# A GRU over 128 steps on one Trainium2 core: the last ten steps' units given out anew, weights of x reloaded into the room of weight sums, and one unit of each period moved behind the projection

## The chip, the core and the metric

The kernel runs on one core of a Trainium2 chip. Its engines work side by side, each on its own queue of instructions: TensorE (PE, matrix products, into PSUM banks), VectorE (DVE), ScalarE (ACT), GpSimd (POOL), and SyncE (SP), which here only issues DMAs. The metric is the device time of one execution in microseconds (us). The profiler also leaves one profiled execution with a trace of every engine.

## The reference

A GRU runs over 128 steps on a batch of 64 sequences with 512 features, in float32; after every fourth step but the last its state goes through one more layer, the projection. The result is added to x.

```python
def step(h, inp):
    x_t, prop = inp
    comb = jnp.concatenate([x_t, h], axis=-1)
    z = jax.nn.sigmoid(comb @ Wz + bz)
    r = jax.nn.sigmoid(comb @ Wr + br)
    comb2 = jnp.concatenate([x_t, r * h], axis=-1)
    h_cand = jnp.tanh(comb2 @ Wh + bh)
    h_new = (1.0 - z) * h + z * h_cand
    h_next = jnp.where(prop, jnp.tanh(h_new @ Wp + bp), h_new)
    return (h_next, h_new)
# prop: (t + 1) % 4 == 0 and t < T - 1; the outputs are the h_new
return x + gru(x, cond_1024, Wz, bz, Wr, br, Wh, bh, Wp, bp)
```

The weights Wz, Wr, Wh have 1024 rows: the upper 512 meet x, the lower 512 meet the state.

## The kernel before

**The recurrent part.** A step t needs three gates, R, Z and H_ (the candidate), and every fourth step (t = 3, 7, ...) the projection P_. The batch is cut into two halves of 32 sequences, h = 0 and 1, and `half(h)` is a generator that emits one half's steps one after the other. A gate of a half is four `products` of 256 columns over the state's transpose (`hT`, or `rhT` for the candidate, `hpT` behind a projection). The chain of a half through a step is: R's products; sigmoid on ACT (L806); r times h and its transpose on DVE (L807, L808); Z's products meanwhile; the candidate's products; tanh on ACT (L846); product with z, subtraction of `keep` and transpose on DVE (L848, L857, L858); in the fourth steps the projection's products, tanh and transpose (L872 to L876). `keep` and the sigmoid of z are made for both halves at once, behind the second half's Z (L818 to L823). A gate's PSUM region is seeded by ACT with the x part and the bias before its products come (`seed`, L368); the seeds of the next step stand on ACT behind the activations that read the regions (L810, L862, L864, L878), and the seed of Z waits for the second half's new state. The loop at L885 to L896 interleaves the halves by the columns that each has emitted, the second one 700 columns behind.

**The x part: units.** x times the upper weights for all steps is work that doesn't hang on the state. It is cut into units and stands in a `queue` (`put`, L383). `fill(n, h)` emits the next n units of a half at three places of a step, given by a triple in `places`: before the candidate's products (`places[0]`, L839), behind the candidate (`places[1]`, L866), and, in the fourth steps, behind the projection (`places[2]`, L880). So the units are what PE does while a chain is on ACT and DVE. Steps 0 to 4 take their triples from HEAD, the last ten from TAIL, the others from PLACES, a period of eight steps that begins with u = (t - 3) % 8 = 0 (steps 11, 19, ..., 115). A half-unit may not be emitted for h = 0 before the unit that frees its bank was emitted for h = 1 (`after` in `fill`).

**Two forms of units.** Most of x goes through a fast scheme of seven products per pair of steps, twice nested, in `batch`. It needs sums and differences of weights: `tw` (made once, read for the products 4, 6 and 7), `tt`, and differences that replace parts of `wx` in place in the first step (`sum_outer_1`, `sum_inner_1`). A batch is 14 units of 192 columns for two products (7 for one), in the order j = 2, 7, 1, 5, 4, 6, 3, in PSUM banks: a (j = 2), x or y (7, later 4 on top), q (1, later 6), r (5, later 3). Behind a bank's last unit stands its reader: `end_x` copies x or y to `cx` on ACT (L507), `end_q` and `end_q2` copy q to `cq` on ACT, `end_r` (L514, L515), `end_q2` (L520) and `end_r2` (L523, L524) add on DVE. Sums on POOL then make the x parts `cp` of the steps (`outer_...`, `pair_left`, `pair_right`). `plain_unit` is the other form: four products of 256 columns per gate and step against the original weights, followed by `add_bias` on DVE (L409). It is used for steps 0 to 3 and for the last two, T - 2 and T - 1.

**The end.** For the plain products of the last two steps, `wx` must hold the original weights again. `reload` (L455) loads rows k = 0 to 2 of it with twelve DMAs on SP in step T - 7 (L840); the rows k = 3 were never replaced, and `plain_last` puts the units with k = 3 first. The four steps from T - 4 on get their x part from two last batches (`pair_left`, `pair_right` with g = LAST, L687 to L690) and from the plain units. `behind_step` adds the state to x in `xr` on POOL (L765), stores finished steps (L775) and loads later x (L90), all on SP.

Of the kernel before, what the change touches and what calls it, by code (L numbers as in the profile page):

```python
# [9 lines left out]
F32 = mybir.dt.float32  # L10
# [8 lines left out]
def kernel(  # L19
# [15 lines left out]
    B, T, D = x.shape  # L35
    H = h0.shape[1]
    P = 128
# [34 lines left out]
    wh = [const.tile([P, K, H], F32, name=f"wh_{i}") for i in range(3)]  # L72
    wp = const.tile([P, K, H], F32, name="wp")

    tw = {n: const.tile([P, S, NQ, 3, J // 2], F32, name=f"tw_{n}") for n in (2, 3, 4)}
    tt = const.tile([P, 7, 3, NQ, 3, J // 4], F32, name="tt")
    gates_in = (Wr, Wz, Wh)

# [139 lines left out]
    def product(ps, h, lT, w, k, start=False):  # L218
        c0, s0 = divmod(k, C)
        products(  # L220
            ps.rearrange("p (d j) -> p d j", d=2),
            h,
            lT[:, c0, s0 * B + h * V : s0 * B + (h + 1) * V],
            lambda c: quarters(w)[:, c, k],
            start,
        )
# [175 lines left out]
    def banks(t):  # L402
        first, second = scratch[:2] if t % 2 == 0 else scratch[2:4]
        return (first[:, : S * J], first[:, S * J :], second[:, : S * J])

    def add_bias(t, gates):
        new_cp(t // 2)
        for i in gates:
            nc.vector.tensor_add(  # L409
                G[t][:, :, :, i, :],  # L410
                banks(t)[i].rearrange("p (h c n) -> p c h n", h=S, c=C),
                bias_x[:, :, :, i, :],
            )

    def plain_unit(t, e, k, start, end=None):
        g, i = divmod(t, Q4)
        bank = (q_bank, q_bank, r_bank) if t % 2 == 0 else (a_bank, a_bank, x_banks[0])
        return (
            lambda h: product(banks(t)[e], h, xT[g][:, i], wx[:, :, e, :], k, start and e != Z),
            S * J,  # L420
            bank[e],
            end,
            bank[1:] if end is not None else (),
        )

    def plain(t):
        order = [(e, k) for e in range(3) for k in range(K)]
        if t == Q4 - 1:
            order = [(e, k) for k in range(K) for e in range(3)]
        return [  # L430
            plain_unit(
                t, e, k, k == 0, (lambda: add_bias(t, (R, Z, H_))) if n == 11 else None
            )
            for n, (e, k) in enumerate(order)
        ]

    def plain_last():
        seq = [
            plain_unit(t, e, 3, True) for t in (T - 2, T - 1) for e in (R, Z, H_)
        ]  # L440
        for t, gates in ((T - 2, (R, Z, H_)), (T - 1, (R, Z)), (T - 1, (H_,))):
            order = [(e, k) for k in (2, 0, 1) for e in gates]
            seq += [
                plain_unit(
                    t,
                    e,
                    k,
                    False,
                    (lambda t=t, gates=gates: add_bias(t, gates)) if (e, k) == order[-1] else None,
                )  # L450
                for e, k in order
            ]
        return seq

    def reload():  # L455
        for i in range(3):
            load_w(wx[:, :, i, :], gates_in[i][:D], 0, 3)

    MB = {}

# [138 lines left out]
    def pair_right(a, p1, x_, g=1):  # L599
# [2 lines left out]


    PLACES = (
        (1, 8, 5), (1, 7, 0), (6, 8, 0), (6, 8, 0), (1, 8, 5), (1, 7, 0), (6, 8, 0), (6, 6, 0),
    )
    HEAD = {0: (12, 12, 0), 1: (8, 6, 0), 2: (16, 12, 0), 3: (8, 6, 8), 4: (6, 8, 0)}
    TAIL = {
        T - 10: (6, 4, 0), T - 9: (3, 8, 0), T - 8: (6, 8, 0), T - 7: (6, 6, 0), T - 6: (0, 4, 0),
        T - 5: (0, 3, 0), T - 4: (0, 3, 0), T - 3: (0, 5, 0), T - 2: (0, 3, 0), T - 1: (0, 0, 0),  # L610
    }

    idle(64)
# [43 lines left out]
    def begin(t):  # L657
        u = (t - 3) % 8
        even = FIRST + 2 * ((t - 3) // 8)
        if t == 0:  # L660
            put(plain(2) + plain(3))
        elif t == 1:
            put(batch((1, 0), [(1, 1), (1, 2)]))
        elif t == 2:
            put(batch((1, 1), [(1, 10), (1, 11)]) + batch((1, 2), [(1, 8), (1, 9)]))
        elif t == 3:
            put(batches(FIRST))
        elif u == 7:
            put(batches(even + 2))
        if t == T - 10:  # L670
            put(
                batch((LAST, 0), [(LAST, 1), (LAST, 2)])
                + batch((LAST, 1), [(LAST, 10)])
                + plain_last()
            )

    def behind_r(t, duo, u):
        odd = FIRST + 2 * duo + 1
        if t == 1:
            for i in (5, 7):  # L680
                sum_inner(i, nc.gpsimd)
                sum_inner_1(i, nc.gpsimd)
        if t == 2:
            pair_left(0, 1, 2)
        elif t == 3:
            pair_right(0, 1, 10)
        if t == T - 7:  # L687
            pair_left(0, 1, 2, LAST)
        elif t == T - 6:
            pair_right(0, 1, 10, LAST)  # L690
        if t == 2:
            sum_inner(4, nc.gpsimd)
            sum_inner_1(4, nc.gpsimd)
        if u == 0 and duo >= 1 and odd - 2 < LAST:
            outer_u2(odd - 2)
# [17 lines left out]
    def behind_step(t, duo, u, h_new):  # L713
        g, j = divmod(t, Q4)
        even, odd = FIRST + 2 * duo, FIRST + 2 * duo + 1
        if t == 0:
            join_x(1, 0)
            join_x(1, 1)
            sum_raw12(1)
        elif t == 3:  # L720
            pair_left(1, 8, 9)
            pair_right(1, 8, 11)

        if duo >= 0:
            if u == 0 and duo >= 1 and odd - 2 < LAST:
                outer_c22(odd - 2)
                outer_c21(odd - 2)
            if even * Q4 < T:
                if u == 0:
                    sum_s34(even)  # L730
                elif u == 1:
                    outer_1(even)
                    outer_c11(even)
                    sum_raw12(odd)
                elif u == 2:
                    outer_u1(even)
                    outer_5(even)
                    sum_raw4(even)
                elif u == 3:
                    outer_c12(even)  # L740
                    outer_u2(even)
                    outer_c22(even)
                    if odd < LAST:
                        sum_s12(odd)
                elif u == 4:
                    if odd < LAST:
                        sum_s34(odd)
                    outer_c21(even)
                    if odd < LAST:
                        outer_1(odd)  # L750
                elif u == 5 and odd < LAST:
                    sum_raw4(odd)
                elif u == 6 and odd < LAST:
                    outer_u1(odd)
                    outer_c11(odd)
                elif u == 7 and odd < LAST:
                    outer_5(odd)
                    outer_c12(odd)
        if duo >= -1 and (even + 2) * Q4 < T:
            if t == 2 or (u == 6 and duo >= 0):  # L760
                sum_raw12(even + 2)
            if u == 7:
                sum_s12(even + 2)
        if t < T - 1:
            nc.gpsimd.tensor_add(xr[g][:, j], xr[g][:, j], h_new)  # L765

        n = 0
        if t >= T - CHUNK:
            n = 3 if t == T - 2 else 0
        elif j == Q4 - 1:  # L770
            n = 4
        if n:
            for h in range(S):
                for q in range(NQ):
                    nc.sync.dma_start(  # L775
                        out=out[ts(h, V), t - n + 1 : t + 1, ts(q, J)],
                        in_=xr[g][part(q), j - n + 1 : j + 1, h, :],
                    )
        if j == 1 and g >= 1 and (g + 1) * Q4 < T:
            new_xr(g + 1)  # L780
            load_x(xr[g + 1], (g + 1) * Q4, Q4)
        if t in (1, 2):
            load_xs(t + 2)
        if duo >= 0:
            if u == 3:
                load_xs(odd + 2)
            elif u == 6:
                load_xs(even + 4)

    def half(h):  # L790

        for t in range(T):
# [13 lines left out]
            crossed(r_, h, R, AF.Sigmoid)  # L806
            nc.vector.tensor_mul(rh[:, h, :], r_, h_old[:, h, :])  # L807
            turn(rhT[:, h, :], rh[:, h, :])  # L808
            if t != 3:
                seed(R, t + 1, h)  # L810
            if last:
                seed(H_, t, h)
# [24 lines left out]
                    for n in range(2, 4):  # L837
                        join_x(2, n)
            yield from fill(places[0], h)  # L839
            if h == 1 and t == T - 7:  # L840
                reload()

            yield from gate(H_, h, rhT, wh[H_])
            h_new = new_two("h", t)
# [15 lines left out]
                nc.scalar.copy(gate_ps(P_, h)[ts(h, 2 * V)], bias_p[ts(h, 2 * V)])  # L860
            elif t < T - 2:
                seed(H_, t + 1, h)  # L862
            if h == 1:
                seed(Z, t + 1, 0)  # L864
            state[t + 1] = h_new, hT
            yield from fill(places[1], h)  # L866
            if h == 1 and t == 0:
                sum_outer_1()
                for i in (1, 2, 3):
                    sum_inner_1(i, nc.vector)  # L870
# [65 lines left out]
```

## Time and profile before

| | |
|---|---|
| runs | 1307.67, 1312.48, 1312.58 us (median 1312.48) |
| profiled execution | 1309.2 us, span from first to last instruction 1307.3 us |
| busy, DVE / ACT / POOL | 59% / 64% / 68% of the span |
| granted TensorE clock, mean | 0.993 |
| a period of eight steps (steps 11/12 to 19/20) | 78.04 us (172.10 to 250.13) |
| reload: first issue to the matmul that waits for it | 1246.89 to 1260.13 us |
| last matmul's end to the end of the span | 1301.44 to 1307.33 us |

In the profile's lines L12 is line 12 of the kernel, times are microseconds unless marked ns, `out<-in` are the program's names without buffer numbers, and a note such as `[0.91 <-ACT cx L497]` says how long the engine was idle before the instruction and which instruction ended that. L204 is the one line in `products` that issues all matmuls of gates, projections and units, so these are told apart by the tile they write: `rec` and `rec_z` for gates and projections, `scratch_q`, `scratch_r`, `scratch_a`, `scratch_x` and `scratch_y` for units.

### The profile page before, as it was taken

What the parts mean: (1) busy time and instruction counts of PE and PEld (TensorE: products, weight loads), DVE (VectorE), ACT (ScalarE), POOL (GpSimd) and SP (SyncE); (2) the same over time, 40 slices, a digit from 0 to 9 for tenths busy, and PEclk for the clock granted to TensorE, in tenths of its full rate; (3) what the DMA queues carried; (4) which work ended last, traced back from release to release, by engine and by line L of the source; (5) the groups of instructions that cost most, each with busy time, mean ns of one, the idle gap of its engine ahead of it and who ended that gap; (6) DMA issues with size and microseconds to landing.
All of it is one profiled execution on the core that took longest, in us unless ns stands there. A gap on an engine that the chain in (4) does not pass through costs nothing.

```text
span 1307.3 us, 60823 instructions
## 1 busy us (share of the span) xinstructions
PE 1263.1 (97%) x26024; PEld 1085.0 (83%) x26024; DVE 774.2 (59%) x2163; ACT 837.9 (64%) x2688; POOL 887.4 (68%) x1030
## 2 busy tenths in 40 slices
PE   7989999999999999999999999999999999999987
PEld 3579988888888888888888888888888888888855
DVE  1646666666665656666666565666656666666534
ACT  1346666666666666666666666666666666666655
POOL 4468767777677776767687676776767787676420
PEclk9989999999999999999999999999999999999999
DMA  8502211112121111211111121111112102111040
GB/s 190 111 19 52 51 35 39 47 35 51 42 61 35 27 46 48 51 36 47 45 30 51 47 56 36 34 48 40 51 36 55 41 25 51 51 36 35 19 107 18
DMA packets 114710, 63.19 MB, mean 48 GB/s; under 512 B 13161, under 2 KB 109673, under 8 KB 114441
## 3 DMA queue, kind: packets, MB, share of 16 engines
q1 hardware_dynamic: 113412, 58.44, 18.0%
q8 instruction: 205, 3.36, 1.1%
q10 hardware_dynamic: 772, 0.72, 0.2%
q14 instruction: 65, 0.52, 0.1%
q0 software_dynamic: 256, 0.14, 0.1%
HBM read 42.47 MB, written 16.78 MB: 45 GB/s over the span
## 4 chain that ended last, share of the span: by engine, by line
PE 88%; DMA 4%; DVE 2%; ACT 2%; SPq 2%; POOL 1%; issue 1%; DVEq 0%; POOLq 0%
PE rec L204 41%; PE rec_z L204 15%; PE scratch_r L204 13%; PE scratch_q L204 9%; PE scratch_a L204 4%; PE scratch_y L204 3%; PE scratch_x L204 3%; DMA xr<-in_x_dram 1%; DVE rec_z L848 1%; DVE h L857 1%; SPq L97 1%; ACT c L230 1%; DMA wx<-in_L_cond_Wz_dram 1%; DMA wh<-in_L_cond_Wr_dram 1%; ACT cx L497 1%
## 5 line engine op out<-in xcount | busy, mean ns | idle before, releaser
L204 PE MATMUL rec<-wh,rhT 128*32 128x256 f32 x4096 | 373.7, 381 | 4.4 <-ACT rec L371 4.4
L204 PE MATMUL rec<-wh,hT 128*32 128x256 f32 x3072 | 277.7, 379 | 2.1 <-DVE hT L233 2.1
L204 PE MATMUL rec_z<-wh,hT 128*32 128x256 f32 x3072 | 278.1, 379 | 0.0
L204 PEld LDWEIGHTS rec<-wh,rhT 128*32 128x32 f32 x4096 | 226.8, 110 | 38.9 <-ACT rec L371 4.8
L230 ACT ACTIVATE scratch_r<-rec 64x128 f32<-64x128 f32 x512 | 128.0, 250 | 146.2 <-PE rec L204 80.7
L371 ACT COPY rec<-cp 64x256 f32<-64x256 f32 x512 | 189.9, 371 | 31.6 <-DVE cp L409 7.7
L230 ACT ACTIVATE rec_z<-rec_z 64x128 f32<-64x128 f32 x512 | 128.0, 250 | 95.8 <-PE rec_z L204 83.6
L204 PEld LDWEIGHTS rec<-wh,hT 128*32 128x32 f32 x3072 | 167.2, 110 | 24.6 <-ACT c L230 3.7
L230 ACT ACTIVATE c<-rec 64x128 f32<-64x128 f32 x512 | 139.3, 272 | 66.8 <-PE rec L204 55.7
L204 PEld LDWEIGHTS rec_z<-wh,hT 128*32 128x32 f32 x3072 | 172.4, 110 | 8.2
L765 POOL TENSOR_TENSOR xr<-xr,h 128x256 f32<-128x256 f32 x127 | 93.2, 734 | 114.3 <-DVE h L857 109.0
L556 POOL TENSOR_TENSOR mb<-mb,mb 128x768 f32<-128x768 f32 x58 | 106.3, 1833 | 68.9 <-DVE mb L524 68.9
L556 POOL TENSOR_TENSOR cp<-mb,mb 128x768 f32<-128x768 f32 x75 | 137.4, 1831 | 5.5 <-DVE mb L524 1.9
L556 POOL TENSOR_TENSOR cp<-mb 128x768 f32<-128x768 f32 x47 | 86.1, 1832 | 56.4 <-ACT rec_z L371 54.9
L514 DVE TENSOR_TENSOR cx<-scratch_r,cx 128x384 f32<-128x384 f32 (+1 forms) x107 | 59.3, 554 | 106.2 <-PE scratch_r L204 97.6
L821 DVE SCALAR_TENSOR_TENSOR keep<-rec_z,h 128x256 f32<-128x256 f32 x96 | 40.8, 425 | 134.2 <-ACT rec_z L230 134.2
L204 PE MATMUL scratch_r<-wx,s12r 128*32 128x192 f32 x1056 | 118.4, 326 | 0.0
L497 ACT COPY cq<-scratch_q 128x384 f32<-128x384 f32 (+1 forms) x214 | 102.4, 478 | 24.9 <-PE scratch_q L204 21.8
L204 PE MATMUL scratch_r<-tw,s 128*32 128x192 f32 x928 | 115.1, 326 | 0.0
L204 PE MATMUL scratch_r<-wx,s 128*32 128x192 f32 x928 | 105.5, 326 | 0.0
L204 PE MATMUL scratch_q<-tt,s 128*32 128x192 f32 x928 | 100.0, 326 | 0.0
L561 POOL TENSOR_TENSOR mb<-mb,bias_x 128x768 f32<-128x768 f32 x35 | 64.2, 1835 | 51.8 <-DVE mb L524 51.8
(155 smaller groups left out, 3517.6 us busy)
## 6 DMA issues: line engine op xcount, KB each, us to landing
out_dram<-xr SPq DMA_DIRECT2D x249, 64.0 KB, 1.8
xr<-in_x_dram SPq DMA_DIRECT2D x248, 64.0 KB, 2.1
xs<-in_x_dram SPq DMA_DIRECT2D x240, 64.0 KB, 2.1
wx<-in_L_cond_Wz_dram SPq DMA_DIRECT2D x4, 256.0 KB, 8.6
wx<-in_L_cond_Wh_dram SPq DMA_DIRECT2D x4, 256.0 KB, 9.9
wh<-in_L_cond_Wr_dram SPq DMA_DIRECT2D x4, 256.0 KB, 8.9
wh<-in_L_cond_Wz_dram SPq DMA_DIRECT2D x4, 256.0 KB, 4.4
wh<-in_L_cond_Wh_dram SPq DMA_DIRECT2D x4, 256.0 KB, 8.1
```

Of the source, the lines that this page charges most:

```text
L97: engs[q % len(engs)].dma_start(out=wt[part(q), k0:k1, :], in_=w[q * P + k0 * V : q * P + k1 * V, :].rearrange("(k e) n -> e k n", e=V),)
L204: nc.tensor.matmul(ps[part(2 * h + c)], lhsT=left, rhs=rhs(c), start=start, stop=True, skip_group_check=True,)
L230: nc.scalar.activation(dst[ts(d, 2 * V)], gate_ps(i, h)[ts(h, 2 * V), d, :], func)
L371: nc.scalar.copy(gate_ps(i, h)[rows].rearrange("p d (c n) -> p d c n", c=C), G[t][rows, :, :, i, :].rearrange("p c d n -> p d c n"),)
L497: nc.scalar.copy(c[:, :nm], ps[:, :nm])
L514: nc.vector.tensor_add(T2[what][:, :nm], r_ps[:, :nm], T2[what][:, :nm])
L556: nc.gpsimd.tensor_add(dst, a, b)
L561: nc.gpsimd.tensor_add(m, m, v.unsqueeze(1).to_broadcast([P, 2, 3 * J]))
L765: nc.gpsimd.tensor_add(xr[g][:, j], xr[g][:, j], h_new)
L821: nc.vector.scalar_tensor_tensor(out=keep, in0=z, scalar=1.0, in1=h_old, op0=ALU.subtract, op1=ALU.mult)
L848: nc.vector.tensor_mul(c, cand[:, h, :], c)
L857: nc.vector.tensor_sub(h_new[:, h, :], c, keep[:, h, :])
```

## The change

Three parts.

1. In PLACES the first step of a period takes its 14 units as (1, 7, 6) in place of (1, 8, 5). It concerns steps 11, 19, ..., 115 (step 3 has a triple in HEAD).
2. The three tiles of `tw` become one, `tw_all`, of the same size. Its room, seen as `again`, takes the reloaded weights k = 0 to 2; `wx` is left as it is. The reload is issued in step T - 9, behind the units that follow the candidate, when the last unit that reads `tw` has been emitted. The plain units of T - 2 and T - 1 read `again` for k < 3 and `wx` for k = 3, in the ordinary order: all of T - 2 (R, Z, H_), then R, H_ and Z of T - 1, each of these with its own `add_bias`.
3. The units of the last steps are given out anew by TAIL, which now begins at T - 11. The sums `pair_left` and `pair_right` move to the end of steps T - 8 and T - 6; the seeds of R for T - 4 move behind the new state of T - 5; the seed of Z for T - 1 moves behind the last units of T - 2.

| step | 117 | 118 | 119 | 120 | 121 | 122 | 123 | 124 | 125 | 126 |
|---|---|---|---|---|---|---|---|---|---|---|
| before | 6, 8, 0 | 6, 4, 0 | 3, 8, 0 | 6, 8, 0 | 6, 6, 0 | 0, 4, 0 | 0, 3, 0 | 0, 3, 0 | 0, 5, 0 | 0, 3, 0 |
| after | 4, 8, 0 | 1, 7, 0 | 1, 7, 5 | 1, 7, 0 | 0, 7, 0 | 0, 7, 0 | 0, 5, 4 | 0, 5, 0 | 0, 5, 0 | 0, 5, 0 |

Steps 119 and 123 have a projection.

```diff
-    tw = {n: const.tile([P, S, NQ, 3, J // 2], F32, name=f"tw_{n}") for n in (2, 3, 4)}
+    tw_all = const.tile([P, 3, S * NQ * 3 * J // 2], F32, name="tw")
+    tw = {
+        n: tw_all[:, n - 2].rearrange("p (a q g u) -> p a q g u", a=S, q=NQ, g=3) for n in (2, 3, 4)
+    }
+    again = tw_all.rearrange("p k (i n) -> p k i n", i=3)
...
+        w = again if t >= T - 2 and k < K - 1 else wx
         return (
-            lambda h: product(banks(t)[e], h, xT[g][:, i], wx[:, :, e, :], k, start and e != Z),
+            lambda h: product(banks(t)[e], h, xT[g][:, i], w[:, :, e, :], k, start and e != Z),
...
-            load_w(wx[:, :, i, :], gates_in[i][:D], 0, 3)
+            load_w(again[:, :, i, :], gates_in[i][:D], 0, K - 1)
...
     PLACES = (
-        (1, 8, 5), (1, 7, 0), (6, 8, 0), (6, 8, 0), (1, 8, 5), (1, 7, 0), (6, 8, 0), (6, 6, 0),
+        (1, 7, 6), (1, 7, 0), (6, 8, 0), (6, 8, 0), (1, 8, 5), (1, 7, 0), (6, 8, 0), (6, 6, 0),
     )
...
-        T - 10: (6, 4, 0), T - 9: (3, 8, 0), T - 8: (6, 8, 0), T - 7: (6, 6, 0), T - 6: (0, 4, 0),
-        T - 5: (0, 3, 0), T - 4: (0, 3, 0), T - 3: (0, 5, 0), T - 2: (0, 3, 0), T - 1: (0, 0, 0),
+        T - 11: (4, 8, 0), T - 10: (1, 7, 0), T - 9: (1, 7, 5), T - 8: (1, 7, 0), T - 7: (0, 7, 0),
+        T - 6: (0, 7, 0), T - 5: (0, 5, 4), T - 4: (0, 5, 0), T - 3: (0, 5, 0), T - 2: (0, 5, 0),
+        T - 1: (0, 0, 0),
...
-                + plain_last()
+                + plain(T - 2)
+                + sum((plain(T - 1, (e,)) for e in (R, H_, Z)), [])
...
-        if t == T - 7:
-            pair_left(0, 1, 2, LAST)
-        elif t == T - 6:
-            pair_right(0, 1, 10, LAST)
...
+        if t == T - 8:
+            pair_left(0, 1, 2, LAST)
+        elif t == T - 6:
+            pair_right(0, 1, 10, LAST)
...
-            if t != 3:
+            if t not in (3, T - 5):
                 seed(R, t + 1, h)
...
-            if h == 1 and t == T - 7:
-                reload()
...
-            if h == 1:
+            if h == 1 and t != T - 2:
                 seed(Z, t + 1, 0)
+            if h == 1 and t == T - 5:
+                for i in range(S):
+                    seed(R, t + 1, i)
             state[t + 1] = h_new, hT
             yield from fill(places[1], h)
+            if h == 1 and t == T - 9:
+                reload()
+            if h == 1 and t == T - 2:
+                seed(Z, t + 1, 0)
```

`plain(t, gates)` builds the list of units for the named gates and hangs `add_bias(t, gates)` on the last one; `plain_last` goes.

## The prediction

> **What bounds the kernel now.** I read the totals first, then what TensorE (PE) waits for, then stretches of equal work against each other, then the order of instructions inside one wait. The page's totals:
> ```profile
> PE 1263.1 (97%) x26024; PEld 1085.0 (83%) x26024; DVE 774.2 (59%) x2163; ACT 837.9 (64%) x2688; POOL 887.4 (68%) x1030
> ```
> The list of PE's waits (who <- whom: us in all, times, longest):
> ```profile
> PE rec L204 <- ACT rec L371: 7.8, 5, 4.4
> PE scratch_x L204 <- ACT cx L497: 6.4, 7, 0.9
> PE scratch_y L204 <- ACT cx L497: 6.4, 7, 0.9
> ```
> PE sets the time: 97% busy. What it can win is its waits, and one kind comes 14 times at 0.9 us: the bank called scratch_x or scratch_y, which ScalarE (ACT) has not yet copied. PE's windows, each from the end of one step's second h (L857) to the next one's (window, length, PE busy, records, granted clock, DMA share, GB/s):
> ```profile
> 1148.42:1159.92 11.50, 11.50 (x248) 1.00 0.10 23
> 1186.58:1199.21 12.63, 11.72 (x249) 1.00 0.23 58
> ...
> 1218.32:1226.53 8.21, 8.21 (x178) 1.00 0.02 5
> 1226.53:1240.43 13.90, 12.26 (x251) 1.00 0.16 40
> 1240.43:1250.16 9.73, 9.73 (x204) 1.00 0.23 58
> 1250.16:1258.30 8.14, 6.73 (x120) 1.00 1.06 231
> 1258.30:1268.89 10.59, 7.97 (x144) 1.00 0.21 47
> 1268.89:1280.64 11.75, 9.26 (x156) 1.00 0.19 47
> 1280.64:1288.12 7.48, 7.48 (x140) 1.00 0.01 2
> 1288.12:1295.56 7.44, 6.67 (x126) 1.00 0.01 2
> ```
> The first two hold the same work (a projection, three gates, 14 units): steps 111/112 and 115/116. The second, behind the first step of a period, is 1.13 us longer. The others are steps 119 to 126. The 1.13 us in order of time (start, length, what):
> ```profile
> 1186.27 0.36 PE L204 MATMUL scratch_q<-wx,xT 128*32 128x192 f32 x2
> 1187.54 0.36 PE L204 MATMUL scratch_y<-tt,xT 128*32 128x192 f32 x2 [0.91 <-ACT cx L497]
> ```
> ACT and, last, VectorE (DVE) in the same stretch:
> ```profile
> 1184.35 0.55 ACT L230 ACTIVATE c<-rec 64x128 f32<-64x128 f32 x2
> 1186.61 0.38 ACT L371 COPY rec_z<-cp 128x256 f32<-128x256 f32 x1 [0.28 <-DVE h L857]
> 1187.01 0.48 ACT L497 COPY cx<-scratch_y 128x384 f32<-128x384 f32 x1
> ```
> ```profile
> 1186.61 0.31 DVE L233 STREAM_TRANSPOSE hT<-h 128x128 f32<-128x128 f32 x1
> ```
> The copy of scratch_y stands on ACT behind the seed of rec_z, which waits for the second half's h. PE's next unit accumulates into that bank and waits for the copy, with everything queued behind it. The projection, which could have run, needs only hT: the first half's since 1185.97, the second's since 1186.92.
>
> **Durations used.** One row (a product of one batch half: 4 PE records) costs 0.215 us at 256 columns (16 records of rec in 0.86) and 0.162 at 192 (scratch_r starts at 1185.74, 1185.91, 1186.07 with a row of scratch_y between). A step without units is 24 rows, 5.17 us; a projection 1.72; a unit of a batch 0.325 (two rows), a unit of a plain product 0.43. From a gate's last row to its activation is 0.3 us (estimate from 1270.1 to 1270.42). From the first half's tanh c to the end of the second half's hT: 2.57 us (1184.35 to 1186.92); to its own hT and the next matmul 1.77 (1266.70 to 1268.47).
>
> **Part 1: 7 units behind the candidate, 6 behind the projection.** Steps 11, 19, ..., 115: 14 steps. A period's unit 8, the one that waits, moves behind the projection. No instruction is added or removed. PE, free at 1186.6, goes on with the first half's projection (hT there for 0.65 us) and the second half's remaining rows; by the order of rows the second half's projection comes 1.13 us later (3 rows of 0.215, 3 of 0.162), at 1187.76, against a hT usable at 1187.07: slack 0.69. The moved unit comes at 1188.4, its bank copied since 1187.5. Behind the projection the chain tanh, transpose, next gate costs 0.3 + 0.55 + 0.03 + 0.31 + 0.15 = 1.34 us; 12 rows cover it (3 of 0.215, 9 of 0.162: 2.1). The last units r3 need DVE's L514: the r5 rows end near 1187.4, L514 takes 0.56, so it is done by 1188.3, and r3 comes near 1189.7. So the whole excess goes: 14 x 1.13 = 15.8 us. From below: PE's shown idle, 14 x 0.91 = 12.7.
>
> **Part 2: the last ten steps.** Work in units is the same (79 from step 117 on), so only waits count. Before, actual length minus work: step 119, 8.21 - (5.17 + 7 x 0.325) = 0.8; 120, 13.90 - 11.44 = 2.5; 121, 0; 122, 8.14 - (5.17 + 6 x 0.43) = 0.4; 123, 10.59 - 6.89 = 3.7; 124, 11.75 - 8.18 = 3.6; 125, 7.48 - 6.46 = 1.0; 126, 0.1; and 1.0 before step 127's first gate. Sum 13.1. In it: 3.2 us idle at 1256.96 for the reloaded weights, and no filler behind the projections of 119 and 123.
> After, three of these go. The reload (12 DMAs on SP, now ahead of the stores of steps 116 to 119) is issued near 1229 and, at the 13.2 us it takes now (1246.89 to 1260.13), is there by 1243, some 20 us before the first plain unit (step 123). It stands on SP behind PE's last read of the old sums in step 119; the stores behind it have until step 123 to free their buffer. The projections get 5 and 4 units. And the 7 units (or 5 plain ones) behind every candidate cover 2.15 to 2.3 us.
> But new waits come, of the kind that part 1 removes, because the units of one batch now fall together behind one candidate. With 0 for the end of the first half's H gate:
> - Steps 118, 120, 122: r5, x4, x4, q6, q6, r3, r3. r3 writes the bank that L514 reads, and L514 stands on DVE behind the second half's hT. c starts at 0.3 to 0.4, hT ends at 2.85 to 3.0, L514 (0.56; 0.36 when one product is in it) ends at 3.3 to 3.6, PE goes on 0.15 later. r3's place is at 1.8 to 1.9. Waits 1.9, 1.7, 1.5.
> - Step 119: a batch of one product, x7, q1, r5, x4: x4 waits for cx as above (c + 2.66 + 0.32 + 0.05 = 3.4, place 1.45: 2.0), then r3 for L514: 0.5.
> - Steps 123 and 124: hT 0.1 late each. From step 125 on the two halves stand next to each other (the H units wait for the R units' end): hT or rhT of the half that ACT serves second is 0.5, 0.45, 0.5 and 0.45 late.
> Sum 9.7, and about 0.13 for each restart (10 waits before: 13.1 by lengths, 11.7 by the gaps themselves): 10.9. Gain 13.1 - 10.9 = 2.2 us. Bounds: 13 (all waits covered) and -2 (each new wait 0.4 longer). I take 2.2, since the same reckoning gives 1.2 for the wait of step 115, where 1.13 was measured. T-5's seeds of R move behind h: three ACT copies (1.1 us) end near 3.8 there, tanh of the projection comes at 4.2, nothing waits. The additions on POOL (2 x 1.83) end some 2 us before the seed that reads them. The end hangs on h of step 126 as before (L765 on POOL, eight stores, L851).
> The granted clock is 1.00 through the 3.17 us of idle at 1257, and the rows after it come at 0.215 as before it, so I price a wait at its length alone.
> The Trainium skill ("TensorE: Matmul & The Clock Gate", part 1, the HAM clock gate) says that an idle window of about 3.4 us halves PE's clock until a busy one. By it a wait of that length would cost up to 1.7 us more (estimate from the page); no wait here is that long, before or after.
>
> **The sum.** 15.8 + 2.2 = 18.0 us off the profiled execution's 1309.2 (span 1307.3 and 1.9 around it): 1291. Its runs were 1307.67, 1312.48 and 1312.58, so the median stands 3.3 above it and gives 1294.5. I say 1293.
>
> **Rivals.**
> - The tail becomes free too: all 13 us go. For it: every place then has 5 units or more. Against: in-order DVE, as just worked out. 1309.2 - 15.8 - 13 = 1280 to 1284.
> - The wait only moves behind the projection. If the next step's R gate, or q6 for cq, waited 1.1 us there, part 1 would give nothing: 1307 to 1310. For it: one unit fewer covers hT. Against: the slacks 0.69 and 0.75.
> - The new waits of the tail are much longer, while part 1 holds at its floor: 1309.2 - 12.7 + 2 = 1298.5, and on the median's level 1302.
> - Slower: a busier PE is granted less clock. Mean now 0.993; each per cent costs 12.6 us of 1263. From 1.9% less on (24.4 us, which takes 1291 to 1315.7) it ends slower; at 0.97, 1320. For it: PE's idle is nearly gone. Against: the granted clock is 1.00 in windows where PE is busy throughout.
>
> **How the numbers follow.** Under 0.5%, 6.5 us, a measurement of this kernel can't tell from no change (its three runs spread 0.4%). The forecast 1286 to 1297: 0.70. Tail free: 0.10. Tail worse, still faster: 0.12. Wait moved: 0.05. Slower: 0.03. So faster 0.92, same 0.05, slower 0.03; range 1284 to 1302.
>
> **What would show it.** Right: the 14 waits of scratch_x and scratch_y for cx gone from the list of PE's waits, the step after a period's first at 11.5 us, no wait of PE on a DMA in the tail, but new waits of scratch_r on cx L514 and of scratch_x on cx L497 in steps 118 to 122, 1.5 to 2.5 us each. Wrong: a wait of rec for hT or hpT 14 times (part 1), a tail without waits, or the clock under 0.99.

## The result and the profile after

| | before | after |
|---|---|---|
| median of the runs | 1311.28 us (1307.67 to 1312.58, 4 runs) | 1295.01 us (1294.84 to 1295.6, 4 runs) |
| profiled execution, its span | 1309.2, 1307.3 us | 1294.84, 1293.1 us |
| the 14 steps behind a period's first, each | 12.63 us | 11.50 us |
| end of step 11 to end of step 116 | 1027.11 us | 1010.93 us |
| the tail: end of step 116 to the end | 108.12 us | 109.87 us |

The kernel is 1.2% faster: ratio 0.9881, 95% interval 0.9859 to 0.9903. By the traces the periods gave 16.2 us. The last eleven steps (the tail), ten of them given out anew, took 1.75 us more.

PE is busy for 98% of the span now. From the list of PE's waits of the changed kernel (who <- whom: us in all, times, longest):

```profile
PE rec L208 <- ACT rec L375: 5.7, 3, 4.4
...
PE scratch_r L208 <- DVE cx L503: 4.2, 4, 1.6
...
PE scratch_x L208 <- ACT cx L486: 1.4, 1, 1.4
```

The 14 waits of scratch_x and scratch_y for cx, 12.8 us, are gone; the one that is left is new, behind the candidate of step 119. New are also the waits of scratch_r for DVE (L503 is L514 of the kernel before). Waits of rec for a seed on ACT (L375, before L371) were there before: four in the tail, behind the projections of steps 119 and 123, 3.4 us in all; the changed kernel has two in its tail, in other places, 1.34 us (the 4.4 is in the first steps of both kernels). No wait on a reloaded weight is left.

PE's windows (window, length, PE busy, records, clock, DMA share, GB/s), each from the end of one step's second h to the next one's. The changed kernel: the step behind a period's first, then steps 119 and 124, the last one, and the whole tail. Then the last step and the tail of the kernel before:

```profile
1171.69:1183.19 11.50, 11.50 (x249) 1.00 0.22 54
...
1200.44:1211.57 11.13, 8.75 (x152) 1.00 0.01 2
...
1251.56:1263.44 11.88, 11.38 (x208) 1.00 0.19 47
...
1279.49:1293.06 13.57, 5.97 (x100) 0.88 0.15 39
1183.19:1293.06 109.87, 95.00 (x1765) 0.99 0.19 47
```

```profile
1295.56:1307.33 11.77, 5.88 (x104) 0.96 0.19 47
```

```profile
1199.21:1307.33 108.12, 92.75 (x1764) 1.00 0.20 47
```

The step behind a period's first is busy throughout. In the tail PE is idle for 14.87 us, where it was idle for 15.37 before. Up to the last step it is idle for less, 7.27 us where it was 9.48; the last step has 1.71 us more, and the time that counts as busy, for the same units, has grown by 2.25 us. Three places of the idle time matter, in order of time.

**Step 119, the seed of R.** PE, ACT and POOL of the changed kernel, one view each:

```profile
1201.38 0.36 PE L208 MATMUL scratch_r<-tw,s 128*32 128x192 f32 x2 [1.57 <-DVE cx L503]
...
1207.08 0.41 PE L208 MATMUL rec<-wh,rhT 128*32 128x256 f32 x2 [0.84 <-ACT rec L375]
...
1210.13 0.52 PE L208 MATMUL scratch_x<-tt,s4r 128*32 128x192 f32 x4
1210.45 0.52 PE L208 MATMUL scratch_q<-tw,xT 128*32 128x192 f32 x4
1212.38 0.36 PE L208 MATMUL scratch_x<-tt,xT 128*32 128x192 f32 x2 [1.40 <-ACT cx L486]
```

```profile
1204.35 0.53 ACT L234 ACTIVATE scratch_r<-rec 64x128 f32<-64x128 f32 x2 [1.15 <-DVE mb L512]
1206.66 0.37 ACT L375 COPY rec<-cp 64x256 f32<-64x256 f32 x1 [1.78 <-POOL cp L545]
1207.05 0.53 ACT L234 ACTIVATE scratch_r<-rec 64x128 f32<-64x128 f32 x2
```

```profile
1204.80 1.82 POOL L545 TENSOR_TENSOR cp<-cp,mb 128x768 f32<-128x768 f32 x1 [4.14 <-DVE mb L513]
```

The last units r3 of a batch now come behind the candidate of step 118. They wait for DVE (1.57 us, forecast 1.9). What was not forecast is what follows: the additions that read them (L512, L513) end late, POOL's sum ends at 1206.62, ACT stands idle for 1.78 us before the seed that reads that sum, and PE's first candidate product waits for the seed, which writes another part of the same PSUM tile. The first sigmoid is late too, 1.15 us behind L512, which reads the tile that it writes; but it isn't what PE waits for: the transpose `rhT` that follows from it ends at 1205.56, the seed at 1207.03.

**Step 123, the moved seeds.** The two seeds of R that moved behind the new state, on ACT, and PE's first product of the projection behind them:

```profile
1251.96 0.76 ACT L375 COPY rec<-cp 64x256 f32<-64x256 f32 x2
```

```profile
1252.38 0.41 PE L208 MATMUL rec<-wp,hT 128*32 128x256 f32 x2 [0.50 <-ACT rec L375]
```

**The end.** ACT in the last step; ACTq is its queue for DMAs:

```profile
1285.41 0.56 ACT L234 ACTIVATE c<-rec 64x128 f32<-64x128 f32 x2 [0.65 <-PE rec L208]
1286.79 1.14 ACTq L841 DMA_DIRECT2D out_dram<-xr  x1
1287.97 0.55 ACT L234 ACTIVATE c<-rec 64x128 f32<-64x128 f32 x2 [2.01 <-issue]
```

The second half's tanh comes first here: by the loop that interleaves the halves by emitted columns, they change places behind the candidate of step 125. Its store is issued by ACT, waits for its data, and is issued ahead of the other half's tanh, which is 2.01 us late. Before, the store stood behind both (there ACT's four pieces of tanh run in one stretch from 1300.89, its store follows at 1303.26).

### The profile page after: what moved, and what is told of

It is laid out like the page before. It is cut to its first block, busy times and chain, and to the rows that moved or that the text cites. A ratio compares the mean times of both kernels' runs of the same rounds, so it can differ in the third digit from the quotient of the medians.

```text
span 1293.1 us, 60850 instructions
## 1 busy us (share of the span) xinstructions
PE 1263.8 (98%) x26024; PEld 1167.3 (90%) x26024; DVE 774.1 (60%) x2163; ACT 835.3 (65%) x2688; POOL 885.9 (69%) x1030
## 4 chain that ended last, share of the span: by engine, by line
PE 92%; DMA 3%; POOL 2%; DVE 1%; SPq 1%; issue 1%; ACT 1%; ACTq 0%; DVEq 0%; POOLq 0%
PE rec L208 42%; PE rec_z L208 15%; PE scratch_r L208 13%; PE scratch_q L208 10%; PE scratch_a L208 5%; PE scratch_x L208 4%; PE scratch_y L208 3%; DMA wh<-in_L_cond_Wr_dram 1%; DMA wh<-in_L_cond_Wh_dram 1%; DMA wx<-in_L_cond_Wz_dram 1%; POOL cp L545 0%; SPq L101 0%; SPq L94 0%; DMA wp<-in_L_cond_Wp_dram 0%; DMA wx<-in_L_cond_Wr_dram 0%
## 5 line engine op out<-in xcount | busy, mean ns | idle before, releaser
L208 PEld LDWEIGHTS rec<-wh,rhT 128*32 128x32 f32 x4096 | 248.3, 110 | 28.4 <-ACT rec L375 6.8
L375 ACT COPY rec<-cp 64x256 f32<-64x256 f32 x512 | 189.8, 371 | 32.3 <-DVE cp L413 6.8
L208 PEld LDWEIGHTS rec_z<-wh,hT 128*32 128x32 f32 x3072 | 191.2, 110 | 7.2
L208 PEld LDWEIGHTS rec<-wh,hT 128*32 128x32 f32 x3072 | 185.7, 110 | 11.9 <-issue 0.6
L208 PE MATMUL scratch_r<-wx,s12r 128*32 128x192 f32 x1056 | 121.9, 326 | 2.3 <-DVE cx L503 2.3
L208 PE MATMUL scratch_r<-tw,s 128*32 128x192 f32 x928 | 120.7, 326 | 1.7 <-DVE cx L503 1.6
L503 DVE TENSOR_TENSOR cx<-scratch_r,cx 128x384 f32<-128x384 f32 (+1 forms) x107 | 59.2, 553 | 85.7 <-PE scratch_r L208 76.6
L208 PE MATMUL scratch_r<-wx,s 128*32 128x192 f32 x928 | 109.7, 326 | 0.0
L208 PE MATMUL scratch_q<-tt,s 128*32 128x192 f32 x928 | 103.5, 326 | 0.0
```

The source lines that it names most:

```text
L208: nc.tensor.matmul(ps[part(2 * h + c)], lhsT=left, rhs=rhs(c), start=start, stop=True, skip_group_check=True,)
L375: nc.scalar.copy(gate_ps(i, h)[rows].rearrange("p d (c n) -> p d c n", c=C), G[t][rows, :, :, i, :].rearrange("p c d n -> p d c n"),)
L503: nc.vector.tensor_add(T2[what][:, :nm], r_ps[:, :nm], T2[what][:, :nm])
```

## The experiments

All medians are to be read with one run in mind. The unchanged kernel, loaded a second time beside itself, gave 1308.57 us against 1312.77 (d0, below), ratio 0.9974 with an interval that leaves 1 out. So medians within 0.3% of each other are not told apart here; where it matters I go by the stretches of the traces, which repeat to 0.2 us (the tail of the kernel before: 108.12 and 108.24).

**One part alone.** e1_period is the kernel before with the first edit only, e2_tail the changed kernel without it:

```diff
-        (1, 8, 5), (1, 7, 0), (6, 8, 0), ...
+        (1, 7, 6), (1, 7, 0), (6, 8, 0), ...
```

> The kernel before with the first step of a period alone at (1, 7, 6). Theory (the two parts add up, the period part gives 1.15 us for each of 14 periods): 16 us off, span near 1291, the step behind a period's first at 11.50 us, the stretch from the second half's h of step 116 to the end 108.1 us as before; so a little faster than the kernel with the whole change (ratio to before near 0.988). Rival (the wait moved is paid back in the tail, or the start differs): under 13 us.

Measured: 1295.05 us, ratio 0.9878 (0.9859 to 0.9896); the step 11.50 us. One number moved from 8 to 7 and one from 5 to 6 is the whole gain.

> The changed kernel with the first step of a period back at (1, 8, 5): the tail's part alone. Theory from the two traces: the stretch from the second half's h of step 116 to the end is 109.9 us against 108.1, so 1 to 2 us slower than before. Rival, the prediction's own figure: 2.2 us faster.

Measured: 1311.72 us, ratio 1.0001 (0.9991 to 1.0012). Its tail is 109.88 us long, as expected. The median does not show the 1.7 us.

**The store at the end.** e3_out_swap is the changed kernel with the two queues of the last stores exchanged:

```diff
-                (nc.sync, nc.scalar)[h].dma_start(
+                (nc.scalar, nc.sync)[h].dma_start(
```

> The changed kernel with the two stores of step 127 on each other's queues: the second half's on SP, the first half's on ACT. Theory: in the changed kernel the second half comes first at the end, its store stands on ACT ahead of the first half's tanh and holds it 2.0 us; swapped, that goes: span 1291.1 to 1291.3, tanh of the first half right behind the other's. Rival (the end hangs on the eight stores of steps 124 to 126): under 0.5 us.

Measured: 1292.82 us, ratio 0.9862 (0.9845 to 0.9878). The tail went from 109.87 to 108.31 us, all of it in the last step (13.57 to 12.01). ACT of this kernel:

```profile
1284.06 1.13 ACT L234 ACTIVATE c<-rec 64x128 f32<-64x128 f32 x4 [0.65 <-PE rec L208]
1286.22 1.14 ACTq L841 DMA_DIRECT2D out_dram<-xr  x1
```

Both halves' tanh (x4) run back to back, the store behind them. 1.56 us, not 2.0: measured from the second half's tanh, the first half's does come 2.0 us earlier, but DVE now multiplies it by z 0.3 us late, behind the second half's addition (at 1285.52, the tanh having ended at 1285.19), and the last store takes 0.1 us longer from its issue to the end (3.93 us on ACT's queue, 3.81 on SP's).

**The reload alone.** e4_reload is the kernel before with the weights reloaded early into the room of the weight sums, and nothing else:

```diff
+        w = again if t >= T - 2 and k < K - 1 else wx
...
-            load_w(wx[:, :, i, :], gates_in[i][:D], 0, 3)
+            load_w(again[:, :, i, :], gates_in[i][:D], 0, K - 1)
...
-            if h == 1 and t == T - 7:
+            if h == 1 and t == T - 8:
```

> The kernel before, with nothing changed but the room of the reloaded weights and the step of the reload (step 120, behind the units ahead of the candidate; 16 us ahead of their use). Theory: the 3.2 us wait for the DMA at step 122 goes, but the first half's hT is then 1.0 us late there, with 4 plain units behind the candidate: 2.3 to 2.5 us off the end. Rivals: 3.4 us off (nothing takes the wait's place), or nothing (DMA hidden anyway).

Measured: 1306.67 us, ratio 0.9963 (0.9952 to 0.9975). By the traces the tail is 104.96 us, 3.16 less than before: the rival's 3.4 is nearer than my 2.4. Only 0.33 us took the place of the reload's wait (PE for hT, at 1259.85, where 1.0 was expected); the other waits for hT are those of before.

**The early reload and the period together.** g1_period_reload is e4_reload with the first edit.

> The kernel before with two of the change's parts only: 7 units behind the candidate and 6 behind the projection in a period's first step, and the weights reloaded early into the room of the weight sums; the old places of the last ten steps. Theory (the two add up): 1311.7 - 16.7 - 5.1, about 1290.0; the tail from the end of step 116 is 105.0 us as with the early reload alone, and no clock below 1.00 in it. Rival (the reload is worth only the 3.2 us of its wait in the profile of the kernel before): 1291.9.

Measured: 1289.82 us, ratio 0.9823 (0.981 to 0.9836); tail 104.83 us. The parts add up, and this kernel, with the old places of the tail, is faster than the changed one.

**The three late things.** b1_three_late is the changed kernel with the seeds of R in two steps moved, and e3's exchange:

```diff
-            if t not in (3, T - 5):
+            if t not in (3, T - 9, T - 5):
                 seed(R, t + 1, h)
...
-                if t == 3:
+                if t in (3, T - 9):
                     for i in range(S):
                         seed(R, t + 1, i)
...
-            if h == 1 and t == T - 5:
-                for i in range(S):
-                    seed(R, t + 1, i)
...
                 crossed(h_next[:, h, :], h, P_, AF.Tanh)
                 turn(hT[:, h, :], h_next[:, h, :])
+                if t == T - 5:
+                    seed(R, t + 1, h)
```

> The changed kernel with three instructions moved, no work added: in step 119 the two seeds of R for step 120 stand on ACT behind the sigmoid of z, in step 123 each half's seed of R stands behind that half's tanh of the projection, and at the end the half that comes second stores by ACT's queue. Theory (the changed kernel's tail lost to three waits that were not foreseen): step 119 goes from 11.13 to about 10.1 us, step 124 (which holds step 123's projection) from 11.88 to about 11.3, the last step from 13.57 to 12.0; the tail from the end of step 116 goes from 109.9 to about 106.7, the median from 1295.0 to about 1291.8. Rival (these waits only cover those of r3 and x4 on the copies, which then take their place): only the last step gains, 1293.2.

Measured: 1293.79 us, ratio 0.9854 (0.9839 to 0.9869), tail 108.25 us. The end gained 1.45, step 124 0.40 (11.48), and step 119 lost 0.25 (11.38). PE of this kernel in step 119:

```profile
1208.85 1.24 PE L208 MATMUL rec<-wh,rhT 128*32 128x256 f32 x14 [1.26 <-ACT rec L375]
```

and ACT:

```profile
1205.89 0.54 ACT L234 ACTIVATE scratch_r<-rec 64x128 f32<-64x128 f32 x2 [0.42 <-DVE rh L798]
...
1208.43 0.77 ACT L375 COPY rec<-cp 64x256 f32<-64x256 f32 x2
```

The second sigmoid came 0.94 us behind the first instead of 2.70, as meant, and it did not help: PE waits for the seed, and I had put the seed still later. My reading that the sigmoid behind the seed was what PE lacked was wrong; it is the seed itself, and what is left to try is an earlier sum on POOL.

**An earlier sum.** c1_r3_early is the changed kernel with four units drawn forward, so that r3 comes ahead of the candidate of step 118:

```diff
-        T - 11: (4, 8, 0), T - 10: (1, 7, 0), T - 9: (1, 7, 5), ...
+        T - 11: (6, 8, 0), T - 10: (6, 4, 0), T - 9: (1, 6, 2), ...
```

> The changed kernel with four units of steps 117 to 119 moved forward: 6 and 8 in step 117, 6 and 4 in step 118, 1, 6 and 2 in step 119; the rest as it is, so the last units r3 of a batch come ahead of the candidate of step 118. Theory (in the changed kernel PE's wait for the seed of R in step 119 begins with r3's place: r3, the addition that reads its bank on DVE, the sum on POOL, the seed): the sum on POOL is done before ACT comes to the seed, PE has no wait for a seed in step 119, the wait of r3 in step 118 is gone too, and steps 117 to 119 take about 26.5 us instead of 28.4 (1.8 and 1.1 off, up to 1 back since two units behind step 119's projection cover less than five). Rival (POOL is late for another reason, the sums it has queued): the seed's wait stays.

Measured: steps 117 to 119 take 26.69 us (28.38 in the changed kernel), PE waits for no seed in step 119, although four units more (1.3 us) lie in that stretch; the tail is 106.65 us (one run, 1291.94 us). In this kernel ACT's view shows no idle time ahead of that seed:

```profile
1204.78 0.37 ACT L375 COPY rec<-cp 64x256 f32<-64x256 f32 x1
```

So the order is r3, DVE, POOL, seed, PE: a unit's place behind the candidate was paid for twice, 1.57 us at its own bank and 0.84 at the seed a step later. Not all of it stays won: in this kernel r3 still waits behind the candidates of steps 120 and 122 (1.48 and 1.61 us), seeds cost 0.76 us behind step 119's projection, and the moved seeds of step 123 cost 1.14 us where they cost 0.50.

**The tail spread otherwise.** a1_spread gives the last ten steps out with more units early and fewer behind the late candidates, and leaves the seeds in their ordinary places:

```diff
-        T - 11: (4, 8, 0), T - 10: (1, 7, 0), T - 9: (1, 7, 5), T - 8: (1, 7, 0), T - 7: (0, 7, 0),
-        T - 6: (0, 7, 0), T - 5: (0, 5, 4), T - 4: (0, 5, 0), T - 3: (0, 5, 0), T - 2: (0, 5, 0),
+        T - 11: (6, 8, 0), T - 10: (6, 4, 0), T - 9: (3, 8, 6), T - 8: (0, 8, 0), T - 7: (0, 6, 0),
+        T - 6: (0, 5, 0), T - 5: (0, 4, 3), T - 4: (0, 4, 0), T - 3: (0, 4, 0), T - 2: (0, 4, 0),
...
-                + sum((plain(T - 1, (e,)) for e in (R, H_, Z)), [])
+                + plain(T - 1, (R, Z))
+                + plain(T - 1, (H_,))
...
-        elif t == T - 6:
+        elif t == T - 7:
             pair_right(0, 1, 10, LAST)
```

> The changed kernel with its last ten steps given out anew: the batches' last units stand ahead of the candidate, nine units fewer behind the candidates of steps 118 to 122, seeds in their ordinary places, the reload in step 118. Same work. By the waits that were foreseen for the changed kernel and now have no place (r3 four times 1.5 to 1.9, x4 2.0) and the three that were not foreseen, some 4 to 5 us of waits are left where the kernel before has 13.1: the tail from the end of step 116 goes from 109.9 to about 99.5 us, the median to about 1284.6. Rival (a plan on paper misses as much here as it did before, some 3.5 us): 1288.

Measured: 1285.1 us, ratio 0.9788 (0.9774 to 0.9801), the best kernel of the study. Its window of the tail and what is left of PE's waits there:

```profile
1183.68:1283.02 99.34, 91.41 (x1765) 0.99 0.20 53
```

```profile
PE rec L208 <- DVE hT L237: 2.1, 6, 0.5
```

(The expectation is wrong in two details: behind the candidates of steps 118 to 122 stand four units fewer, of 118 to 126 eight, not nine; and the reload stands in step 119 as in the changed kernel, issued at 1203.59 us.) The tail is 10.5 us shorter than the changed kernel's, with the same number of records on PE. No wait for a bank or a seed is left in it.

**The clock behind the reload.** e1_period's profile has a tail of 109.70 us, though its last steps are those of the kernel before (108.12). PE waits for the weights in both. Behind the wait, the kernel before (window, length, PE busy, records, clock, DMA share, GB/s):

```profile
1256.00:1260.00 4.00, 0.89 (x12) 1.00 1.02 212
...
1262.00:1264.00 2.00, 2.00 (x44) 1.00 0.04 8
```

and e1_period:

```profile
1240.00:1244.00 4.00, 1.18 (x16) 1.00 1.10 214
1244.00:1246.00 2.00, 1.61 (x28) 0.90 0.41 98
1246.00:1248.00 2.00, 2.00 (x27) 0.50 0.03 8
1248.00:1250.00 2.00, 2.00 (x35) 0.75 0.00 0
```

The granted clock is halved for some 3 us, 27 records run where 44 do, and the tail is 1.6 us longer. To see what this does to the runs, d1_warm puts matmuls that nobody reads into the wait:

```diff
+    def warm(n):
+        for i in range(n):
+            for q in range(NQ):
+                nc.tensor.matmul(
+                    scratch[4][part(q), : S * J],
+                    lhsT=wh[0][:, 0, :V],
+                    rhs=wh[0][:, 0, : S * J],
...
+            if h == 0:
+                warm(13)
+            unit[0](h)
```

> The kernel before with 52 matmuls of 256 columns into an unused bank (13 rows, about 2.8 us by 0.215 each) put on PE just ahead of the unit that waits for the reloaded weights in step 122. They lie in the 3.2 us of the wait, so by themselves they cost nothing and save nothing. Theory (in some executions the idle of 3.2 us lets PE's clock fall to half for 3.3 us after it, as in the profile of the period change alone, which costs 1.6 us): PE is never idle over 1 us there, the clock stays 1.00 in every profile, and the median goes down by 0.5 to 1.6 us against the kernel before, the slowest runs by 1.6. Rival (the spread of the kernel before comes from its first 60 us alone): the same median within 0.3 us.

Measured: 1312.35 us, ratio 1.0001 (0.9991 to 1.001). The premise failed: the 52 matmuls took 5.6 us, since two of them, not four, take the 0.215 us of a row, and the tail became 110.6 us; the clock stayed 1.00, and 2.5 us more of work left the median where it was. So half of them, d2_warm_half (`warm(6)`), and beside it the kernel before once more, d0_before_again:

> The kernel before with 24 instead of 52 matmuls ahead of the unit that waits for the weights (52 took 5.6 us, since one row is only two of them: 24 should take 2.6 us and end inside the wait of 3.2). Theory (in most executions of the kernel before the clock falls behind that wait): the clock stays 1.00 there, the tail from the end of step 116 is 108.1 us or less, the runs lie as close together as with 52 (within 3 us), and since 52 gave the median of the kernel before with 2.5 us more work, 24 give about 2.5 us less than it: ratio 0.998. Rival (the 52 matmuls cost nothing for another reason, say that the weights came later in those runs): ratio 1.000.

Measured: 1309.86 us, ratio 0.9977 (0.9963 to 0.999); the matmuls took 2.80 us, the tail 108.26 us, the clock stayed 1.00.

> The kernel before, unchanged, for a second profile of it. Theory: PE waits 3.2 us for the weights as before, and in this execution the granted clock is more likely than not at 0.5 for 3 us or more behind that wait; then steps 122 and 123 together take 20.4 us or more instead of 18.7, and the tail from the end of step 116 109.7 or more instead of 108.1. If the clock stays 1.00 again, 18.7 and 108.1 come back. Rival (the runs differ in the first 60 us alone): 108.1 whatever the total.

Measured: 1308.57 us, ratio 0.9974 (0.9962 to 0.9986) against the same kernel; PE's wait again 3.18 us, the clock again 1.00 behind it, tail 108.24 us. So d2's gain proves nothing, since the unchanged kernel had the same. What is shown is that the clock can fall behind that wait (one profile of three in which the wait was left as it was). How often it does, and whether that makes the runs of the kernel before lie 5 us apart (1308.54 to 1313.65 beside e1 to e4) where those of the kernels with the early reload lie 0.8 to 3.2 apart, stays open.

Two things on record narrow it. Each run comes with the mean granted clock of its core, and the time goes with it: of the 46 runs of the kernel before beside all experiments, those up to 1309.80 us have 0.992 to 0.995, those from 1313.13 us on 0.988 to 0.990. The six runs of d0, of the same kernel, have 0.991 to 0.993, so their lower median goes with the clock too. And the wait for the weights isn't the only place where the clock can fall: in the first steps PE has two waits, of 1.69 and 0.96 us, that end at 53.92 and 55.73 us in the kernel before (1.68 and 0.96 in e2_tail, at 53.90 and 55.70), and behind them e2_tail has

```profile
56.00:58.00 2.00, 2.00 (x30) 0.50 0.00 0
```

and the kernel before

```profile
56.00:58.00 2.00, 2.00 (x56) 1.00 0.04 8
```

(e4_reload has 0.52 there.) In which of the runs without a trace the clock fell, and behind which wait, is not on record.

## Why the prediction was right, and where it was not

- **Part 1** (forecast 15.8, measured 16.2 between the ends of steps 11 and 116, 15.8 of it in the 14 steps and the rest in hundredths of the others). The wait of scratch_y and scratch_x went and nothing took its place; the step came out at 11.50 us. e1_period shows that this edit alone makes the result.
- **Part 2, the size of one term**: "Gain 13.1 - 10.9 = 2.2 us" measured -1.75. This is the term that was mis-sized, by 4 us, and it is why the profiled execution is at 1294.84 and not at the sum's 1291. That the median, 1295.01, lies so near to the 1294.5 that the sum gave for it is luck: the sum takes the medians to stand 3.3 above the profile, and here they stand 0.2 above it, so two misses of nearly the same size cancel.
- **The waits that were foreseen** are there, but shorter by PE's idle time: r3 in steps 118, 120 and 122, 1.57, 1.33 and 0.96 (forecast 1.9, 1.7, 1.5); x4 1.40 (2.0), r3 behind it 0.32 (0.5); for hT and rhT two of 0.2 to 0.25 (2.1 in all). Together 6.0 us where 9.7 was the forecast. A restart adds 0.2 to 0.3 by the starts of the matmuls, where the prediction took 0.13.
- **The waits that were not foreseen** are one part of the miss. "The additions on POOL (2 x 1.83) end some 2 us before the seed that reads them" is wrong for step 119: r3's place made L513 late, the sum came 1.78 us after ACT was free for the seed, and PE lost 0.84 (c1 has neither). "T-5's seeds of R move behind h: ... nothing waits" is wrong: it looked at tanh on ACT, and it was PE's projection, in the same tile, that waited 0.50 (b1 gave 0.40 back). "The end hangs on h of step 126 as before" is wrong: the prediction had the halves side by side from step 125 on, they had changed places, and the store on ACT's queue cost 1.56 (e3). That is 2.9 us, some 3.4 with restarts.
- **The other part stays open.** Since the foreseen waits were shorter, the unforeseen ones don't add up to the 4 us by themselves. PE's busy time in the tail grew from 92.75 to 95.00 us on the same units (a1_spread: 91.41), which a reckoning in waits can't show. One place of it stands above: just before the wait for cx in step 119, four records of 192 columns take 0.32 us (scratch_x at 1210.13 to scratch_q at 1210.45) instead of the 0.162 of "Durations used". That one half's rows run alone there would explain it; no run separates it.
- **The reload** is worth nearly its whole wait by the trace: 3.16 us off the tail (e4). The new places of the units, with the seeds and sums moved along with them, therefore cost 4.9 us against e4's tail of 104.96.
- **The price of an idle PE.** "I price a wait at its length alone" held in two profiles of the kernel before and failed in e1_period's, where 2.90 us of idle, with 0.31 shortly before, halved the clock for some 3 us; at the start of e2_tail even two waits of 1.68 and 0.96 us did. ("No wait here is that long" overlooks the 4.4 us in the first steps, which its own list shows; the forecast does not hang on it.)
- The Trainium skill ("TensorE: Matmul & The Clock Gate", Part 1: The HAM clock gate) says that the window of some 3.4 us in which idleness is counted runs freely, so that where a stretch of work falls in it differs from run to run. The traces agree as far as they go: nearly the same idle did (e1_period) and did not (3.17 and 3.18 us) halve the clock. The prediction had read the page's 3.4 us as a length below which a wait is safe; e1_period's is shorter, so here the measurement decides: 3.4 us is no such bound.
- **The rivals.** Of "the new waits of the tail are much longer" the price came true, 1.75 us where it has 2, but not the reason (the foreseen waits were shorter), and part 1 did not fall to its floor of 12.7. "The wait only moves behind the projection" is refuted by the window without idle time. A slower clock did not come (0.992 against 0.993; in that rival 1291 and 24.4 make 1315.4, not 1315.7, on which nothing rests). "The tail becomes free too" was not what this change does, but it can be had: a1_spread's 1285.1 us lies 1 us above that rival's 1280 to 1284.

## What to carry to other kernels

A unit of filler work has two prices: the wait at its own bank, and what its result is needed for later; follow both to the next reader on the critical path, across every engine in between, before you move it. Where instructions share a PSUM tile, a seed for the next step can hold up a matmul of this one. And when the order of two interleaved streams flips, look at what each of them has on an in-order queue, a store's issue among it.

## What the runs showed of the hardware that was not expected

- TensorE's clock fell to 0.50 behind an idle stretch of 2.90 us in one profile, and stayed at 1.00 behind 3.17 and 3.18 us in two others of the same wait. Behind two waits of 1.68 and 0.96 us, 0.8 us apart, it fell to 0.50 in e2_tail's profile; in that of the kernel before it stayed at 1.00 behind the same two.
- A store issued by ACT holds ACT's next activation until the store's data is there and its issue (1.14 us) is over: 2.01 us here.
- Two copies of one kernel on the same chip differed by 0.3% in their medians (1308.57 us in 6 runs, 1312.77 in 14), and the quicker one ran at the higher mean clock.
